# A batch-normalised outer product on one core: long rows stored in halves, part of their finishing moved to ScalarE and GpSimd, short rows moved to VectorE

## The chip, the core and the metric

The kernel runs on one core of a Trainium2 chip. A core has a matrix engine (PE), three engines for elementwise work, VectorE (DVE), ScalarE (ACT) and GpSimd (POOL), and a queue processor (SyncE, SP) that here issues the stores. SBUF is the working memory of 128 partitions; PSUM is a smaller memory that GpSimd does not use in this kernel. Sixteen DMA engines move data between SBUF and the chip's main memory (HBM). Instructions of one engine run in their order; engines wait for each other through semaphores.

The metric is the device time of one launch in microseconds. Before the change it is 1891.26 us, the median of 3 runs (1891.12 to 1891.61).

## The reference

`xi` and `xj` are 1024 x 39 x 16 floats. For each of the 741 pairs (r, c) with c < r the outer product of xj's feature r and xi's feature c is formed, normalised over the batch and the 16 x 16 entries, scaled by gamma and beta of the pair, and multiplied by a matrix W.

```python
rows, cols = np.tril_indices(39, k=-1)          # 741 pairs
cross = xj[:, rows, :, None] * xi[:, cols, None, :]           # 1024 x 741 x 16 x 16
mean = jnp.mean(cross, axis=(0, 2, 3), keepdims=True)
var = jnp.mean(jnp.square(cross - mean), axis=(0, 2, 3), keepdims=True)
normed = (cross - mean) * jax.lax.rsqrt(var + 1e-5)
normed = normed * gamma[None, :, None, None] + beta[None, :, None, None]
out = normed[:, :, None, :, :] * W[None, None, :, :, :]
```

The output holds 1024 x 741 x 256 floats, 777 MB; the inputs are 5 MB. For each pair the normalisation is one factor s and one summand t: out = (s * cross + t) * W.

## The kernel before

**Setup.** The batch is laid over the 128 partitions, 8 entries on each (NT = 8). From sums and products of xi and xj, without forming any pair, the kernel works out s and t of all pairs (lines 249 to 427); `apply` (line 423) combines them with gamma and beta, group of rows by group of rows, and leaves s in `st_sb[:, 0]` and t in `st_sb[:, 1]` (SBUF). `w_dve` is a copy of W in PSUM for VectorE, `w_sb` the one in SBUF for GpSimd.

**Tiles.** A row r has the r pairs (r, 0) to (r, r-1). A tile is one row for two of the 8 batch entries of each partition (T = 2), 2 x r x 256 floats a partition. `tiles` (lines 62 to 71) lists row 19 first, then for r = 20 to 38 and each of the four batch pairs the row r and its partner 38 - r, together 76 KB a partition. The buffer `y_sb` has two halves of that size, used in turn; a row and its partner share a half. Row 38 has no partner.

**A tile's way.** From the third tile on (the loop at line 438):

- `scale_xi` (line 155): GpSimd multiplies xi by s into a small buffer `xs`, of which there are two. It is issued two tiles ahead.
- `products` (line 167): for each of the two batch entries and each i of 16, one instruction multiplies `xs` by the scalar xj[r, i] and writes 16 of the 256 entries of all r pairs. Of the 16, ScalarE takes 12 and GpSimd 4; for rows over TWO = 31, ScalarE 11 and GpSimd 5. They write into `y_sb`, so they wait until the stores of what lay there have landed.
- `finish` (line 219): for all but the last pairs of the row, VectorE does t and W in one instruction a pair (line 238). The last 13% of the pairs, rounded, are GpSimd's: it adds t pair by pair (line 226) and multiplies all of them by W at once (line 230).
- `store` (line 175): SyncE issues the store when its pairs are finished. `bounds` (line 212) cuts a row into pieces: one for rows to ONE = 24, two for rows to TWO = 31, three above; the first eight tiles have cuts of their own. The last piece of a row over 24 goes as two stores, one for each batch entry, so that the products of the first entry can begin before the second has left.

The program's order on each engine is the order in the file: `finish` of tile n, then `products` of tile n + 1. The first two tiles take another way: products of raw xi, then s and t in one instruction (`affine`, line 186), then W on VectorE (`weigh`, line 200).

The step that the change touches on the long rows:

```python
split = r - int(r * POOL_SHARE + 0.5)
for c in range(split, r):
    nc.gpsimd.tensor_scalar(y[:, :, c, :], ..., t_c, 1.0, ALU.add, ALU.mult)
nc.gpsimd.tensor_tensor(y[:, :, split:r, :], ..., w_sb, ALU.mult)
```

Of the kernel before, what the change touches and what calls it, by code (L numbers as in the profile page):

```python
# [7 lines left out]
F32 = mybir.dt.float32  # L8
AF = mybir.ActivationFunctionType
ALU = mybir.AluOpType  # L10
# [4 lines left out]
T = 2  # L15


ONE, TWO = 24, 31
FIRST_PIECES = (
    (0, 2, 5, 9, 14, 19), (0, 6, 12, 19), (0, 4, 11, 19), (0, 9, 19), (0, 10, 20), (0, 9, 18), (0, 10, 20), (0, 9, 18)  # L20
)


POOL_I, POOL_I_LONG = 4, 5
POOL_SHARE = 0.13

LOADS = (0, 1, 2, 4, 8)


ROW_GROUPS = (  # L30
# [5 lines left out]
def tile_pair_outer_batchnorm(  # L36
# [15 lines left out]
    nc = tc.nc  # L52
    P = nc.NUM_PARTITIONS
    NB, F, E = xi.shape
    NT = NB // P
    EE = E * E
    NP = F * (F - 1) // 2
    first = [r * (r - 1) // 2 for r in range(F)]
# [5 lines left out]
    tiles = [(mid, t0, t0 // T * half // 2) for t0 in range(0, NT, T)]  # L64
# [8 lines left out]
    RAW = 2  # L73

    cpool = ctx.enter_context(tc.tile_pool(name="cpool", bufs=1))
    scaled = ctx.enter_context(tc.tile_pool(name="scaled", bufs=2))
    psp = ctx.enter_context(tc.tile_pool(name="ps", bufs=1, space=bass.MemoryType.PSUM))
    xi_sb = cpool.tile([P, NT, F, E], F32, name="xi_sb")
    xj_sb = cpool.tile([P, NT, F, E], F32, name="xj_sb")
    w_sb = cpool.tile([P, 1, EE], F32, name="w_sb")  # L80
    st_sb = cpool.tile([P, 2, NP], F32, name="st_sb")
    s_sb = st_sb[:, 0:1].unsqueeze(3)
    t_sb = st_sb[:, 1]
# [39 lines left out]
    banks = [psp.tile([P, 512], F32, name=f"ps{n}") for n in range(7)]  # L123
    ps_s, ps_c, ps_g = banks[0], banks[1], banks[2:5]

    ps_st = banks[5:7] + ps_g
    stt = nc.vector.scalar_tensor_tensor

    def view(n):
        r, _, u = tiles[n]  # L130
        return y_sb[:, u : u + T * r, :].rearrange("p (t n) e -> p t n e", t=T)

    def product(n, engine, t, i, src):

        r, t0, _ = tiles[n]
        y = view(n).rearrange("p t n (i j) -> p t n i j", j=E)[:, t, :, i, :]
        scale = xj_sb[:, t0 + t, r, i : i + 1]
        if engine is nc.scalar:
            nc.scalar.activation(y, src, AF.Copy, scale=scale)  # L139
        else:  # L140
            engine.tensor_scalar(y, src, scale, 1.0, ALU.mult, ALU.mult)  # L141
# [12 lines left out]

    def scale_xi(n):
        r, t0, _ = tiles[n]
        n0 = first[r]
        xs = scaled.tile([P, T, r, E], F32, tag="xs", name=f"xs_{r}_{t0}")
        nc.gpsimd.tensor_tensor(  # L159
            xs,  # L160
            xi_sb[:, t0 : t0 + T, 0:r, :],
            s_sb[:, :, n0 : n0 + r, :].to_broadcast([P, T, r, E]),
            ALU.mult,
        )
        xs_of[n] = xs

    def products(n):

        xs = xs_of.pop(n)
        split = E - (POOL_I_LONG if tiles[n][0] > TWO else POOL_I)  # L170
        for t in range(T):
            for i in range(E):
                product(n, nc.scalar if i < split else nc.gpsimd, t, i, xs[:, t])

    def store(n, c0, c1):
        r, t0, _ = tiles[n]
        n0 = first[r]

        step = 1 if r > ONE and c1 == r else T
        for t in range(0, T, step):  # L180
            nc.sync.dma_start(  # L181
                out_v[:, t0 + t : t0 + t + step, (n0 + c0) * EE : (n0 + c1) * EE],
                view(n)[:, t : t + step, c0:c1, :].rearrange("p t n e -> p t (n e)"),
            )

    def affine(n):

        r = tiles[n][0]
        y = view(n)
        for c in range(r):  # L190
            s_c = st_sb[:, 0, first[r] + c : first[r] + c + 1]
            t_c = t_sb[:, first[r] + c : first[r] + c + 1]
            if c % 2 == 0:
                nc.scalar.activation(y[:, :, c, :], y[:, :, c, :], AF.Identity, bias=t_c, scale=s_c)  # L194
            else:
                nc.gpsimd.tensor_scalar(  # L196
                    y[:, :, c, :], y[:, :, c, :], s_c, t_c, ALU.mult, ALU.add
                )

    def weigh(n):  # L200

        y = view(n)
        for c0, c1 in zip(bounds(n), bounds(n)[1:]):
            nc.vector.tensor_tensor(  # L204
                y[:, :, c0:c1, :],
                y[:, :, c0:c1, :],
                w_dve.unsqueeze(1).to_broadcast([P, T, c1 - c0, EE]),
                ALU.mult,
            )
            store(n, c0, c1)  # L210

    def bounds(n):
        if n < len(FIRST_PIECES):
            return FIRST_PIECES[n]
        r = tiles[n][0]
        pieces = 1 + (r > ONE) + (r > TWO)
        return tuple(q * r // pieces for q in range(pieces + 1))

    def finish(n):

        r = tiles[n][0]
        n0 = first[r]
        y = view(n)
        split = r - int(r * POOL_SHARE + 0.5)
        for c in range(split, r):
            nc.gpsimd.tensor_scalar(  # L226
                y[:, :, c, :], y[:, :, c, :], t_sb[:, n0 + c : n0 + c + 1], 1.0, ALU.add, ALU.mult
            )
        if split < r:
            nc.gpsimd.tensor_tensor(  # L230
                y[:, :, split:r, :],
                y[:, :, split:r, :],
                w_sb.unsqueeze(1).to_broadcast([P, T, r - split, EE]),
                ALU.mult,
            )
        for c0, c1 in zip(bounds(n), bounds(n)[1:]):
            for c in range(c0, min(c1, split)):
                stt(  # L238
                    y[:, :, c, :],
                    y[:, :, c, :],  # L240
                    t_sb[:, n0 + c : n0 + c + 1],
                    w_dve.to_broadcast([P, T, EE]),
                    ALU.add,
                    ALU.mult,
                )
            store(n, c0, c1)

    with tc.manual_schedule():
        for t0, t1 in zip(LOADS, LOADS[1:]):
            nc.sync.dma_start(xj_sb[:, t0:t1], xj_v[:, t0:t1])  # L250
# [157 lines left out]
        for r0, r1, bank, _ in ROW_GROUPS:  # L408
            n0, n1 = first[r0], first[r1 - 1] + r1 - 1
            at = used[bank]  # L410
            used[bank] = at + 2 * (n1 - n0)
            ps = ps_st[bank][:, at : used[bank]].rearrange("p (x n) -> p x n", x=2)
# [10 lines left out]
        def apply(group):  # L423
            ps, n0, n1 = spread_of[group]
            nc.vector.tensor_mul(ps[:, 1], ps[:, 1], st_sb[:, 0, n0:n1])
            nc.vector.tensor_mul(st_sb[:, 0, n0:n1], ps[:, 0], st_sb[:, 0, n0:n1])
            nc.vector.tensor_add(st_sb[:, 1, n0:n1], ps[:, 1], st_sb[:, 1, n0:n1])

        apply(0)
        affine(0)  # L430
        weigh(0)
        scale_xi(2)
        affine(1)
        weigh(1)
        apply(2)
        apply(1)

        for n in range(1, len(tiles)):
            if n == 1:
                products(2)  # L440
                scale_xi(3)
                continue
            if n + 2 < len(tiles):
                scale_xi(n + 2)
            finish(n)
            for group, (_, _, _, tile_of) in enumerate(ROW_GROUPS):
                if n == tile_of:
                    apply(group)
            if n + 1 < len(tiles):
                products(n + 1)  # L450
# [28 lines left out]
```

## Time and profile before

| | |
|---|---|
| time of the runs (median of 3) | 1891.26 us |
| the profiled execution's own time | 1891.05 us |
| its span (first to last instruction) | 1889.3 us |
| VectorE busy | 1730.7 us, 92% of the span |
| ScalarE busy | 1621.3 us, 86% |
| GpSimd busy | 1574.5 us, 83% |
| matrix engine busy | 24.5 us, 1% |
| time of the packets on the store queue | 98.3% of 16 engines' span |
| written to HBM | 777 MB, 414 GB/s with the reads over the span |
| stores issued | 305 |

Busy time is read as follows: an engine's instructions overlap a little, so the mean duration of VectorE's line 238, 740 ns, is more than their spacing; eleven of them in a row took 7.32 us, 0.67 us each. "Idle before, and releaser" names what ended a wait: line 139 on ScalarE waited 171.8 us in total for stores to land, in 58 waits. "issue" means that the profile shows nothing waited for. A slice of the page is a fortieth of the span, 47.2 us.

### The profile page before, as it was taken

The page shows a single profiled execution, that of the slowest core. Times are in us where ns is not written, and L with a number is a line of the kernel's source. Part 1 is how long each engine was busy: PE and PEld are TensorE (multiplying, and loading weights), DVE is VectorE, ACT ScalarE, POOL GpSimd, SP SyncE. Part 2 cuts the span into 40 slices and gives each one's busy share as a digit, 9 for nine tenths or more (in the row PEclk, how much of TensorE's full clock was granted, in tenths as well). Part 3 has the DMA queues.
Part 4 walks back from the last instruction along what each step waited for, and adds up shares of the span by engine and source line. Part 5 has one row for each costly group of instructions (what it writes and reads, how often), then busy time and mean ns, then how long its engine had stood idle before and what let it go on. Part 6 is the DMA issues. An engine that isn't in the chain of part 4 may idle for free. (4 is left out here: it accounts for less than half of the span.)

```text
span 1889.3 us, 10288 instructions
## 1 busy us (share of the span) xinstructions
PE 24.5 (1%) x128; PEld 23.1 (1%) x128; DVE 1730.7 (92%) x2612; ACT 1621.3 (86%) x3625; POOL 1574.5 (83%) x1985
## 2 busy tenths in 40 slices
PE   3100000000000000000000000000000000000000
PEld 3100000000000000000000000000000000000000
DVE  7999999998989898989898989899999999999996
ACT  8999989898989898989898989888888888888762
POOL 9798878788888888888888888888888888888972
DMA  4999999999999999999999999999999999999999
GB/s 164 390 418 429 425 427 429 430 424 429 424 425 426 424 424 426 422 425 425 424 425 423 426 423 426 422 422 422 421 421 422 418 415 419 416 419 419 415 419 390
DMA packets 70288, 783.67 MB, mean 415 GB/s; under 512 B 5057, under 2 KB 6209, under 8 KB 15937
## 3 DMA queue, kind: packets, MB, share of 16 engines
q1 hardware_dynamic: 69632, 780.46, 98.3%
q10 hardware_dynamic: 576, 2.56, 0.3%
q14 instruction: 79, 0.64, 0.1%
q8 instruction: 1, 0.02, 0.0%
HBM read 6.00 MB, written 776.99 MB: 414 GB/s over the span
## 5 line engine op out<-in xcount | busy, mean ns | idle before, releaser
L238 DVE SCALAR_TENSOR_TENSOR y_sb<-y_sb,st_sb,w_dve 128x512 f32<-128x512 f32 x2542 | 1678.5, 740 | 131.5 <-issue 128.3
L139 ACT ACTIVATE y_sb<-xs,xj_sb 128x256 f32<-128x256 f32 (+32 forms) x3544 | 1576.4, 539 | 223.5 <-DMA out_dram<-y_sb 171.8
L141 POOL TENSOR_SCALAR y_sb<-xs,xj_sb 128x560 f32<-128x560 f32 (+35 forms) x1256 | 643.2, 536 | 35.1 <-DMA out_dram<-y_sb 32.6
L230 POOL TENSOR_TENSOR y_sb<-y_sb,w_sb 128x1024 f32<-128x1024 f32 (+4 forms) x138 | 442.0, 3203 | 11.5
L159 POOL TENSOR_TENSOR xs<-xi_sb,st_sb 128x576 f32<-128x576 f32 (+37 forms) x150 | 187.8, 1252 | 225.3 <-ACT y_sb L139 217.8
L226 POOL TENSOR_SCALAR y_sb<-y_sb,st_sb 128x512 f32<-128x512 f32 x384 | 259.4, 692 | 12.9 <-ACT y_sb L139 12.9
L204 DVE TENSOR_TENSOR y_sb<-y_sb,w_dve 128x2560 f32<-128x2560 f32 (+5 forms) x8 | 21.0, 2682 | 2.3 <-ACT y_sb L194 2.3
L139 ACT ACTIVATE y_sb<-xi_sb,xj_sb 128x304 f32<-128x304 f32 x40 | 18.7, 534 | 0.1
L414 PE MATMUL ps<-y_sb 39*128 39x38 f32 (+37 forms) x76 | 16.5, 397 | 5.6 <-DVE y_sb L402 5.6
L414 PEld LDWEIGHTS ps<-y_sb 39*128 39x128 f32 x76 | 16.3, 329 | 5.8 <-issue 5.8
L194 ACT ACTIVATE y_sb<-y_sb,st_sb 128x512 f32<-128x512 f32 x20 | 14.2, 797 | 0.0
L196 POOL TENSOR_SCALAR y_sb<-y_sb,st_sb 128x512 f32<-128x512 f32 x18 | 13.5, 771 | 0.3 <-issue 0.3
L141 POOL TENSOR_SCALAR y_sb<-xi_sb,xj_sb 128x304 f32<-128x304 f32 x24 | 11.9, 518 | 0.0
L299 DVE TENSOR_REDUCE y_sb<-y_sb 128x78 f32<-128x1248 f32 x8 | 11.1, 1442 | 0.0
L277 DVE TENSOR_REDUCE y_sb<-xj_sb 128x78 f32<-128x1248 f32 (+1 forms) x5 | 5.9, 1189 | 5.6 <-DMA xj_sb<-in_r_xj_dram 5.6
L293 ACT ACTIVATE y_sb<-y_sb 128x1248 f32<-128x1248 f32 x8 | 9.9, 1243 | 1.3 <-POOL y_sb L283 1.1
L283 POOL TENSOR_TENSOR y_sb<-xj_sb,y_sb 128x1248 f32<-128x1248 f32 x4 | 9.3, 2314 | 1.9 <-ACT y_sb L327 1.9
L283 POOL TENSOR_TENSOR y_sb<-xi_sb,y_sb 128x1248 f32<-128x1248 f32 x4 | 9.3, 2318 | 0.0
L316 PE MATMUL ps<-y_sb 128*39 128x79 f32 x48 | 7.2, 339 | 16.5 <-DVE y_sb L299 16.5
L316 PEld LDWEIGHTS ps<-y_sb 128*39 128x39 f32 x48 | 6.1, 183 | 17.4 <-DVE y_sb L299 9.6
L277 DVE TENSOR_REDUCE y_sb<-xi_sb 128x78 f32<-128x1248 f32 (+1 forms) x5 | 5.9, 1186 | 0.0
L259 POOL TENSOR_SCALAR_AFFINE_SELECT y_sb<-y_sb 39x4992 f32<-39x4992 f32 x1 | 4.6, 4623 | 0.0
(45 smaller groups left out, 16.9 us busy)
## 6 DMA issues: line engine op xcount, KB each, us to landing
out_dram<-y_sb SPq DMA_DIRECT2D x32, 3072.0 KB, 13.7
out_dram<-y_sb SPq DMA_DIRECT2D x28, 2816.0 KB, 15.7
out_dram<-y_sb SPq DMA_DIRECT2D x32, 1664.0 KB, 14.2
out_dram<-y_sb SPq DMA_DIRECT2D x16, 3328.0 KB, 17.2
out_dram<-y_sb SPq DMA_DIRECT2D x30, 1536.0 KB, 15.2
out_dram<-y_sb SPq DMA_DIRECT2D x12, 3840.0 KB, 17.6
out_dram<-y_sb SPq DMA_DIRECT2D x12, 3584.0 KB, 18.1
out_dram<-y_sb SPq DMA_DIRECT2D x22, 1792.0 KB, 17.4
```

Of the source, the lines that this page charges most:

```text
L139: nc.scalar.activation(y, src, AF.Copy, scale=scale)
L141: engine.tensor_scalar(y, src, scale, 1.0, ALU.mult, ALU.mult)
L159: nc.gpsimd.tensor_tensor(xs, xi_sb[:, t0 : t0 + T, 0:r, :], s_sb[:, :, n0 : n0 + r, :].to_broadcast([P, T, r, E]), ALU.mult,)
L194: nc.scalar.activation(y[:, :, c, :], y[:, :, c, :], AF.Identity, bias=t_c, scale=s_c)
L196: nc.gpsimd.tensor_scalar(y[:, :, c, :], y[:, :, c, :], s_c, t_c, ALU.mult, ALU.add)
L204: nc.vector.tensor_tensor(y[:, :, c0:c1, :], y[:, :, c0:c1, :], w_dve.unsqueeze(1).to_broadcast([P, T, c1 - c0, EE]), ALU.mult,)
L226: nc.gpsimd.tensor_scalar(y[:, :, c, :], y[:, :, c, :], t_sb[:, n0 + c : n0 + c + 1], 1.0, ALU.add, ALU.mult)
L230: nc.gpsimd.tensor_tensor(y[:, :, split:r, :], y[:, :, split:r, :], w_sb.unsqueeze(1).to_broadcast([P, T, r - split, EE]), ALU.mult,)
L238: stt(y[:, :, c, :], y[:, :, c, :], t_sb[:, n0 + c : n0 + c + 1], w_dve.to_broadcast([P, T, EE]), ALU.add, ALU.mult,)
L283: nc.gpsimd.tensor_tensor(devs[n % 7], sources[x][:, t0 : t0 + T], shift[:, x : x + 1, :].unsqueeze(3).to_broadcast([P, T, F, E]), ALU.sub ...
L316: nc.tensor.matmul(acc[0:F, 0 : 2 * F + 1], lhs, fb[:, t], start=t == 0, stop=t == NT - 1)
L414: nc.tensor.matmul(ps[:, :, first[r] - n0 : first[r] - n0 + r], pick[:, r, :], stq[:, :, 0:r], start=True, stop=True,)
```

## The change

Four things are changed together.

1. `TWO` goes: rows over 24 are all cut in two pieces, so rows 32 to 38 leave in halves and not in thirds. The limit from which GpSimd takes 5 of 16 products moves from 31 to `LONG` = 33.
2. Rows over 33: the GpSimd pairs are no longer the last ones but the last eight of the first half (`p0` to `p1`), in two groups of four. ScalarE adds t to them, one instruction a pair; GpSimd multiplies each group by W. VectorE does all others.
3. Rows of up to 4 pairs (`SHORT`): `scale_xi` is left out; VectorE multiplies xi by s and forms the products, one instruction for each batch entry, and no pair is left to GpSimd.
4. For that, s and xj are also kept in PSUM: `apply` now leaves s in PSUM too and copies it to `st_sb` with an instruction of its own, and one ScalarE copy during setup puts xj of rows 1 to 4 into PSUM (`xj_short`).

```diff
-ONE, TWO = 24, 31
+ONE, LONG = 24, 33
-POOL_SHARE = 0.13
+POOL_SHARE, POOL_PAIRS_LONG = 0.13, 8
+SHORT = 4
...
+    s_short = ps_g[0]
+    xj_short = ps_c.rearrange("p (t r i) -> p t r i", t=NT, i=E)
...
     def scale_xi(n):
         r, t0, _ = tiles[n]
+        if r <= SHORT:
+            return
...
     def products(n):
+        r, t0, _ = tiles[n]
+        if r <= SHORT:
+            xs = scaled_short.tile([P, T, r, E], F32, tag="xs_short", name=f"xs_{r}_{t0}")
+            nc.vector.tensor_tensor(
+                xs,
+                xi_sb[:, t0 : t0 + T, 0:r, :],
+                s_short[:, first[r] : first[r] + r]
+                .unsqueeze(1)
+                .unsqueeze(3)
+                .to_broadcast([P, T, r, E]),
+                ALU.mult,
+            )
+            for t in range(T):
+                nc.vector.tensor_tensor(
+                    view(n)[:, t].rearrange("p n (i j) -> p n i j", j=E),
+                    xs[:, t].unsqueeze(2).to_broadcast([P, r, E, E]),
+                    xj_short[:, t0 + t, r - 1 : r, :].unsqueeze(3).to_broadcast([P, r, E, E]),
+                    ALU.mult,
+                )
+            return
         xs = xs_of.pop(n)
-        split = E - (POOL_I_LONG if tiles[n][0] > TWO else POOL_I)
+        split = E - (POOL_I_LONG if tiles[n][0] > LONG else POOL_I)
...
-        pieces = 1 + (r > ONE) + (r > TWO)
+        pieces = 1 + (r > ONE)
...
     def finish(n):
-        split = r - int(r * POOL_SHARE + 0.5)
-        for c in range(split, r):
-            nc.gpsimd.tensor_scalar(
-                y[:, :, c, :], y[:, :, c, :], t_sb[:, n0 + c : n0 + c + 1], 1.0, ALU.add, ALU.mult
-            )
-        if split < r:
+        long = r > LONG
+        p1 = r // 2 if long else r
+        p0 = p1 - (POOL_PAIRS_LONG if long else int(r * POOL_SHARE + 0.5) if r > SHORT else 0)
+        step = POOL_PAIRS_LONG // 2 if long else r
+        for c0 in range(p0, p1, step):
+            c1 = min(c0 + step, p1)
+            for c in range(c0, c1):
+                t_c = t_sb[:, n0 + c : n0 + c + 1]
+                if long:
+                    nc.scalar.activation(y[:, :, c, :], y[:, :, c, :], AF.Identity, bias=t_c)
+                else:
+                    nc.gpsimd.tensor_scalar(
+                        y[:, :, c, :], y[:, :, c, :], t_c, 1.0, ALU.add, ALU.mult
+                    )
             nc.gpsimd.tensor_tensor(
-                y[:, :, split:r, :],
-                y[:, :, split:r, :],
-                w_sb.unsqueeze(1).to_broadcast([P, T, r - split, EE]),
+                y[:, :, c0:c1, :],
+                y[:, :, c0:c1, :],
+                w_sb.unsqueeze(1).to_broadcast([P, T, c1 - c0, EE]),
                 ALU.mult,
             )
         for c0, c1 in zip(bounds(n), bounds(n)[1:]):
-            for c in range(c0, min(c1, split)):
+            for c in [*range(c0, min(c1, p0)), *range(max(c0, p1), c1)]:
                 stt(
...
         def apply(group):
             ps, n0, n1 = spread_of[group]
             nc.vector.tensor_mul(ps[:, 1], ps[:, 1], st_sb[:, 0, n0:n1])
-            nc.vector.tensor_mul(st_sb[:, 0, n0:n1], ps[:, 0], st_sb[:, 0, n0:n1])
+            nc.vector.tensor_mul(ps[:, 0], ps[:, 0], st_sb[:, 0, n0:n1])
+            nc.vector.tensor_copy(st_sb[:, 0, n0:n1], ps[:, 0])
             nc.vector.tensor_add(st_sb[:, 1, n0:n1], ps[:, 1], st_sb[:, 1, n0:n1])
 
         apply(0)
         affine(0)
+        nc.scalar.copy(xj_short, xj_sb[:, :, 1 : SHORT + 1, :])
         weigh(0)
```

In the built order this makes the products of rows 1 to 4 stand on VectorE after the long partner's pairs, and the eight adds on ScalarE directly after the row's own products. Rows 32 to 38 issue one store fewer a tile.

More of the change, by code (lines that the diff above doesn't have):

```diff
@@ L75, in tile_pair_outer_batchnorm @@
     cpool = ctx.enter_context(tc.tile_pool(name="cpool", bufs=1))
+    scaled_short = ctx.enter_context(tc.tile_pool(name="scaled_short", bufs=1))
     scaled = ctx.enter_context(tc.tile_pool(name="scaled", bufs=2))
```

## The prediction

> **What bounds the kernel now.** I read the page's slices first: is anything full?
>
> ```profile
> DVE  7999999998989898989898989899999999999996
> ACT  8999989898989898989898989888888888888762
> DMA  4999999999999999999999999999999999999999
> GB/s 164 390 418 429 425 427 429 430 424 429 424 425 426 424 424 426 422 425 425 424 425 423 426 423 426 422 422 422 421 421 422 418 415 419 416 419 419 415 419 390
> ```
>
> The DMA engines are full from the second slice on; VectorE is close behind. GB/s falls late, at full DMA. So I asked for busy time and rate in stretches that hold whole rows: 22 to 24, 25 to 31, 32 to 37, and 38 (columns: stretch, its length, busy us by engine, clock, DMA share, GB/s).
>
> ```profile
> 283.40:564.20 280.80, 0.00 (x0) 0.00 (x0) 262.01 (x399) 254.67 (x576) 233.77 (x300) 1.00 1.00 427
> 564.20:1224.00 659.80, 0.00 (x0) 0.00 (x0) 609.33 (x924) 592.47 (x1341) 547.15 (x703) 1.00 1.01 424
> 1224.00:1794.20 570.20, 0.00 (x0) 0.00 (x0) 520.10 (x788) 470.72 (x1076) 497.70 (x627) 1.00 1.00 419
> 1794.20:1888.20 94.00, 0.00 (x0) 0.00 (x0) 74.36 (x113) 41.39 (x60) 49.97 (x47) 1.00 0.97 409
> ```
>
> A unit is a row r and its partner 38-r, two batches each: 76 KB a partition, 9.96 MB. Per batch and partition it leaves in 2, 3 and 4 contiguous stretches in the first three windows, in 3 in the last. The times at which each store's completion lands in the trace, taken over whole rows, give per unit 23.40 us (rows 22 to 24), 23.56 us (25 to 31; single rows 23.41 to 23.69), 23.76 us (32 to 37; 23.68 to 23.86), 23.52 us (row 38). The rate follows the number of stretches.
>
> Then what has to keep that queue full: the chain of waits (start, length, what) in row 37, and the timeline there.
>
> ```profile
> 1742.58 3.88 ACT y_sb L139 x6
> 1746.46 0.21 issue
> 1746.67 1.98 ACT y_sb L139 x3
> 1748.65 5.93 DVE y_sb L238 x9
> 1754.64 11.12 DMA out_dram<-y_sb
> ...
> 1765.87 4.75 ACT y_sb L139 x7
> ```
>
> ```profile
> 1742.58 19.81 ACT L139 ACTIVATE y_sb<-xs,xj_sb 128x592 f32<-128x592 f32 x46 [4.50 <-DMA out_dram<-y_sb]
> ...
> 1757.73 10.62 DVE L238 SCALAR_TENSOR_TENSOR y_sb<-y_sb,st_sb,w_dve 128x512 f32<-128x512 f32 x16 [2.49 <-issue]
> ...
> 1760.03 3.35 POOL L226 TENSOR_SCALAR y_sb<-y_sb,st_sb 128x512 f32<-128x512 f32 x5
> 1763.46 5.62 POOL L230 TENSOR_TENSOR y_sb<-y_sb,w_sb 128x2560 f32<-128x2560 f32 x1
> ```
>
> It is a ring of two halves of y: a landing frees a half (1742.5), ScalarE's 22 products take 15 us, VectorE starts when they are done (1757.73), a third of the row is stored, that store waits in the queue. I call slack the time by which a first third's issue comes before the queue would run dry: landing of the store ahead, minus end of the issue, minus 1.8 us (the first store of all, into an empty queue, landed 3.25 us after its issue, of which its packets are 1.44). From the trace: row 32 7.3 to 8.4 us, 34 5.8 to 6.9, 35 5.2 to 5.9, 36 3.2 to 4.3, 37 2.5 to 3.4, row 38's four tiles 2.6, 2.3, 2.1, 1.4. Slack is thin exactly where the change works.
>
> **What the Trainium skill says.** "DMA: Bandwidth & Descriptors", Why small descriptors are slow, gives each packet a fixed overhead beside its bytes; the trace agrees: median packets take 427 ns for 11,264 B, 841 ns for 22,528 B, so two of the small cost 13 ns more than one of the large. "SBUF — State Buffer", Who interferes with whom: a VectorE instruction with at most one SBUF input doesn't contend with GpSimd; both new VectorE multiplies take the other input from PSUM, and line 238, built so, keeps 0.66 us a pair while GpSimd works. "ScalarE: Activation LUTs", What ACT_TABLE_LOAD costs, prices a per-partition pointer operand at some 93 ns: here 797 ns with two against 708 with one, same size.
>
> **Part by part.** Prices, from the groups by shape (busy us, mean ns of one):
>
> ```profile
> L230 POOL TENSOR_TENSOR y_sb<-y_sb,w_sb 128x2048 f32<-128x2048 f32 x10 | 45.1, 4513 | 0.8
> L194 ACT ACTIVATE y_sb<-y_sb,st_sb 128x512 f32<-128x512 f32 x20 | 14.2, 797 | 0.0
> L139 ACT ACTIVATE y_sb<-xs,xj_sb 128x512 f32<-128x512 f32 x29 | 18.0, 708 | 4.2 <-DMA out_dram<-y_sb 4.2
> ```
>
> And from the timeline of the start:
>
> ```profile
> 63.96 11.28 DVE L238 SCALAR_TENSOR_TENSOR y_sb<-y_sb,st_sb,w_dve 128x512 f32<-128x512 f32 x17 [1.44 <-ACT y_sb L139]
> ```
>
> *Halves instead of thirds, rows 32 to 38.* 7 rows x 8 batches x 128 partitions = 7,168 packets of 63,744 go, and 28 of 305 stores. By landings: 24 units x (23.76 - 23.56) + 4 x (23.52 - 23.40) = 5.3 us. By packets: row 38 had 465 + 2 x 502 ns; 19,456 B lies between 691 (18,432 B) and 766 (20,480 B), so 2 x 728; 12 ns less, 16 packets an engine and unit: 0.20 us x 28 = 5.6 us. By the windows: 24 x (23.77 - 23.49), from 9.96 MB at 419 and 424 GB/s, and 4 x (23.49 - 23.33) for row 38 at the rates of three and two stretches, 7.4 us, but they count bytes of engines that run ahead. I take 5.4; ends 3.5 and 7.4.
>
> *Eight pairs of rows 34 to 38.* The t-add moves from GpSimd to ScalarE: 8 a tile at 0.62 (one pointer, 18.0/29) to 0.71 us (14.2/20), say 5.2 us. GpSimd's weighing goes from one of 5 pairs (5.6, after 3.35 of adds) to two of 4 (4.51 each): 9.0 before, 9.0 after. VectorE is spared 3 to 4 pairs a tile, 0.66 us each. The chain matters: in the first half 4 adds (2.6) and two multiplies (9.0) with hand-overs make 11.8 us after the products; before, the first third was 12 x 0.66 = 7.9 us. So 3.9 later (4.5 in rows 34 and 35). Against it: the products of a half start when batch 0 of the last piece has landed, and what drains after that is batch 1 of 19 pairs, not 13: 6 x 128 KB, 1.9 us earlier (1.5 in row 34). Net 2.0 us later (3.0 and 2.6). Slack left: row 34 about 3, 35 about 2.9, 36 1.7, 37 1.0, row 38 0.6, 0.3, 0.1, -0.6. I charge 0.7 us. Behind the adds on ScalarE stand the next products: 22 x 0.67 + 5.2 = 20 us of 23.6, free in time.
>
> *Rows 32, 33.* 16 pairs before the first store instead of 10 or 11 (+3.3 to 4.0 us), one more ScalarE product a batch (+0.6 each), start 1.5 earlier: about 3.7 of 6.6 to 8.4 us slack. Nothing.
>
> *Rows 1 to 4.* ScalarE loses 24 products of 0.22 us (5.2 us: it pays for the adds), GpSimd 8. VectorE gains, for r = 4, one multiply of 128 and two of 1,024 elements (line 204 took 1,220 ns for 1,024): 2.7 us, and a pair of t and W (0.66), against 4 pairs spared (2.6). For r = 1 about 1.1 against 2. Equal; its gap of 2.49 us a unit covers it. They stand behind the long row's stores; the queue holds over 9 us then.
>
> *Setup.* A ScalarE copy of 512 elements before the second tile: 0.6 us by the product of that size. VectorE has weighing to do until 61.2, but at 63.96 it waits for ScalarE's products, and the store that follows (issue ended 67.21, store ahead landed 68.13) finds no slack: +0.6. Six extra copies in apply, 0.18 to 0.41 us by the multiplies of their shapes: the first lies under ScalarE's products (till 39.13), two under the 1.44 us wait, three where VectorE idles: +0.1, ends 0 and 0.9.
>
> Sum: -5.4 + 0.7 + 0.6 + 0.1 = -4.0. Span 1889.3 to 1885.3; the profiled execution itself 1891.05 to 1887.05; the median of the runs is 0.2 above that: **1887.2 us**, its own range 1884.6 to 1889.3.
>
> **Rivals.** *Gain half eaten*: hand-overs cost 0.9 us more a tile, rows 37 and 38 starve. A late first half delays every second unit (the other ring half then has the surplus): two payments a row, some 2 us: 1889.2. For it the thin slack; against it row 38 now, which runs on 1.4 to 2.6 us and still makes 23.52. *No gain in rate*: rows 32 to 37 are slow because the queue runs low, not for packets; then only +1.4: 1892.7. Against it DMA share 1.00 and slack above 5 in rows 32 to 34, as slow as the rest. *Slower*: the chain from ScalarE to GpSimd, twice over, decides. If it takes d longer than 11.8 us, each row pays 2 x (d - slack): for d = 2.7 that is 2 x (1.0 + 1.7 + 2.6) for rows 36, 37, 38, some 10.6 in place of 0.7: 1897. The sign turns at d = 1.7 (a multiply of 5.4 us instead of 4.51), 0.2% slower at 2.35. For it: spans on GpSimd are rough, and this chain was never on the path; against it 4.51 is the same shape in the same kernel. *The change does nothing*: excluded: in the built order rows 32 to 38 have one store fewer a tile, and the short rows' products stand on VectorE.
>
> **How the numbers follow.** Forecast 0.66, half eaten 0.12, no gain 0.06, slower chain 0.16. About 0.2% (3.8 us) is what a measurement here can tell. The forecast's middle lies just beyond it, so I count three fifths of that case as faster and the rest, with the two cases between, as no change: faster 0.40, same 0.44, slower 0.16. Range: the forecast's low end, and up to where half the slow case is in: 1884.5 to 1895.
>
> **What would show it.** Right: GB/s of the last nine slices near 424; about 62,000 packets on the first queue (69,632 - 7,168 - 28 x 16); line 267 at 4.5 us; first halves issued 0 to 3 us ahead of need; DMA share under 1 only in row 38. Wrong: line 267 above 5.3 us, or ScalarE's wait for the landing gone while VectorE waits longer; DMA slices below 9 from 1420 us on; or a rate that stays at 419 with a full queue.

## The result, and the profile after

The changed kernel takes 1885.37 us, the median of 6 runs (1885.22 to 1885.50); the kernel before took 1891.19 us on the same chip (6 runs, 1891.06 to 1891.61). The ratio is 0.9969, with a 95% interval of 0.9956 to 0.9982: 5.8 us or 0.31% less, a little more than the 0.2% that the prediction set as its bound. It forecast 1887.2 us, in a range of 1884.5 to 1895. The profiled execution took 1885.49 us, with a span of 1883.8.

First the slices of the page after the change, and the line of the store queue (packets, MB, share of 16 engines).

```profile
DVE  7999999998989898989898989898999999988885
ACT  8999989898989898989898989898988888888883
DMA  4999999999999999999999999999999999999999
GB/s 162 386 420 424 428 428 426 431 424 425 431 423 426 424 426 423 425 424 425 426 423 425 423 426 425 416 425 423 419 421 427 421 428 421 423 419 418 424 416 413
...
q1 hardware_dynamic: 62016, 780.46, 98.2%
```

The DMA engines are as full as before, and VectorE is less full at the end (8 where there was 9). The last nine slices run at 413 to 428 GB/s, 420 on average, where they ran at 390 to 419, 414 on average; the prediction named 424 as the sign of being right, and four of the last five slices stay short of it. The queue carries 62,016 packets, 7,616 fewer than before. Then busy time and rate in stretches that hold whole rows: 25 to 31, 32 to 37 and 38 (columns: stretch, its length, busy us of PE, PEld, DVE, ACT and POOL, clock, DMA share, GB/s).

```profile
564.20:1224.00 659.80, 0.00 (x0) 0.00 (x0) 608.65 (x923) 594.28 (x1344) 545.09 (x700) 1.00 1.01 424
1224.00:1790.00 566.00, 0.00 (x0) 0.00 (x0) 520.64 (x793) 483.17 (x845) 451.92 (x401) 1.00 1.00 422
1790.00:1882.00 92.00, 0.00 (x0) 0.00 (x0) 64.25 (x98) 54.01 (x80) 48.23 (x33) 1.00 0.99 423
```

Rows 25 to 31, which leave as they did, keep their 424. Rows 32 to 37 go from 419 to 422. Row 38 shows 409 before and 423 here, but the window before runs to the last landing and this one stops 0.9 us short of it: over the whole row, 1789.4 to 1882.9 us, it is 418. ScalarE has 12 us more to do in rows 32 to 37, GpSimd 46 us less.

The difference can be placed to a tenth of a microsecond with the times at which the stores' completions land in the trace, per unit (a row, its partner and two batches; 4 units a row). A row ends when the last of the 16 DMA engines has completed its last store:

| | before | after | difference in all |
|---|---|---|---|
| rows 25 to 31, us a unit | 23.564 | 23.560 | 28 x -0.004 = -0.1 |
| rows 32 to 37, us a unit | 23.760 | 23.537 | 24 x -0.223 = -5.4 |
| row 38, us a unit | 23.515 | 23.383 | 4 x -0.132 = -0.5 |
| last landing of row 19, us | 94.60 | 95.20 | +0.6 |
| end of the span after the last landing, us | 1.09 | 0.85 | -0.2 |

Together -5.6, which is the difference of the spans (1889.34 and 1883.78) within rounding (rows 20 to 24 add less than 0.1). So nearly all that was won was won where the rows leave in halves; the start lost 0.6. Row 38's 0.5 is the least certain part, since its end before is set by one engine that landed 1.1 us behind the other 15.

The timeline in row 37 shows the new hand-overs (start, length, what, count, wait and its releaser).

```profile
1736.19 15.05 ACT L145 ACTIVATE y_sb<-xs,xj_sb 128x592 f32<-128x592 f32 x22 [2.85 <-DMA out_dram<-y_sb]
...
1747.63 0.75 DVE L190 TENSOR_TENSOR y_sb<-xs,ps 128x256 f32<-128x256 f32 x2
...
1751.34 13.92 DVE L275 SCALAR_TENSOR_TENSOR y_sb<-y_sb,st_sb,w_dve 128x512 f32<-128x512 f32 x21 [2.17 <-ACT y_sb L145]
1751.34 5.01 ACT L262 ACTIVATE y_sb<-y_sb,st_sb 128x512 f32<-128x512 f32 x8
1754.04 9.02 POOL L267 TENSOR_TENSOR y_sb<-y_sb,w_sb 128x2048 f32<-128x2048 f32 x2 [4.44 <-ACT y_sb L262]
```

When the 22 products are done (1751.24), ScalarE adds t to eight pairs in 5.01 us; GpSimd starts after four of them, at 1754.04, and is done at 1763.06. The first half can be issued 11.8 us after the products, as the prediction had it. The short partner, row 1, sits on VectorE just before. The groups by shape over rows 34 to 38 (busy us, mean ns of one, idle before):

```profile
L267 POOL TENSOR_TENSOR y_sb<-y_sb,w_sb 128x2048 f32<-128x2048 f32 x40 | 180.1, 4525 | 94.5 <-ACT y_sb L262 94.5
L262 ACT ACTIVATE y_sb<-y_sb,st_sb 128x512 f32<-128x512 f32 x156 | 97.7, 708 | 1.8
...
L190 DVE TENSOR_TENSOR y_sb<-xs,ps 128x1024 f32<-128x1024 f32 x8 | 9.4, 1218 | 0.1
```

The chain of waits in the same stretch of row 37 (start, length, what) has the order that it had before: weighing on VectorE, with the short row behind it, a landing, ScalarE's products.

```profile
1740.84 6.66 DVE y_sb L275 x10
1747.50 0.03 DVE xs L180
1747.53 11.83 DMA out_dram<-y_sb
...
1759.46 6.52 ACT y_sb L145 x10
```

The shares have moved, though: from 1715 to 1790 us the chain is 45% ScalarE's products, 37% VectorE's pairs and 16% stores, where from 1720 to 1800 us before it was 31, 27 and 42%. The ring has less room than it had.

The slack of the first piece (the prediction's measure) fell as the halves and the chain through GpSimd imply: row 34 from 5.8-6.9 to 2.1-3.3 us, 36 from 3.2-4.3 to 1.2-2.6, 37 from 2.5-3.4 to 0.3-1.9, and row 38 from 2.6, 2.3, 2.1, 1.4 to 0.6, 1.2, -0.8, -0.4.

### The profile page after: what moved, and what is told of

Its sections match the earlier page's. It is cut to its first block, busy times and chain, and to the rows that moved or that the text cites. A ratio compares the mean times of both kernels' runs of the same rounds, so it can differ in the third digit from the quotient of the medians.

```text
span 1883.8 us, 9616 instructions
## 1 busy us (share of the span) xinstructions
PE 24.5 (1%) x128; PEld 23.1 (1%) x128; DVE 1721.6 (91%) x2606; ACT 1648.8 (88%) x3418; POOL 1524.4 (81%) x1741
## 3 DMA queue, kind: packets, MB, share of 16 engines
q1 hardware_dynamic: 62016, 780.46, 98.2%
## 5 line engine op out<-in xcount | busy, mean ns | idle before, releaser
L275 DVE SCALAR_TENSOR_TENSOR y_sb<-y_sb,st_sb,w_dve 128x512 f32<-128x512 f32 x2482 | 1640.5, 741 | 131.0 <-issue 117.7
L145 ACT ACTIVATE y_sb<-xs,xj_sb 128x320 f32<-128x320 f32 (+20 forms) x3176 | 1503.1, 566 | 192.2 <-DMA out_dram<-y_sb 165.4
L147 POOL TENSOR_SCALAR y_sb<-xs,xj_sb 128x352 f32<-128x352 f32 (+25 forms) x1112 | 597.8, 561 | 41.0 <-DMA out_dram<-y_sb 36.4
L267 POOL TENSOR_TENSOR y_sb<-y_sb,w_sb 128x2048 f32<-128x2048 f32 (+3 forms) x154 | 509.4, 3313 | 104.0 <-ACT y_sb L262 94.5
L167 POOL TENSOR_TENSOR xs<-xi_sb,st_sb 128x576 f32<-128x576 f32 (+33 forms) x134 | 182.7, 1364 | 185.2 <-ACT y_sb L145 179.1
L264 POOL TENSOR_SCALAR y_sb<-y_sb,st_sb 128x512 f32<-128x512 f32 x284 | 192.1, 692 | 0.1
L262 ACT ACTIVATE y_sb<-y_sb,st_sb 128x512 f32<-128x512 f32 x160 | 100.2, 708 | 1.9
L190 DVE TENSOR_TENSOR y_sb<-xs,ps 128x1024 f32<-128x1024 f32 (+3 forms) x32 | 24.8, 817 | 0.5
L222 ACT ACTIVATE y_sb<-y_sb,st_sb 128x512 f32<-128x512 f32 x20 | 14.3, 798 | 0.0
L224 POOL TENSOR_SCALAR y_sb<-y_sb,st_sb 128x512 f32<-128x512 f32 x18 | 13.5, 763 | 0.6 <-issue 0.6
```

Of the source, the lines that this page charges most:

```text
L167: nc.gpsimd.tensor_tensor(xs, xi_sb[:, t0 : t0 + T, 0:r, :], s_sb[:, :, n0 : n0 + r, :].to_broadcast([P, T, r, E]), ALU.mult,)
L190: nc.vector.tensor_tensor(view(n)[:, t].rearrange("p n (i j) -> p n i j", j=E), xs[:, t].unsqueeze(2).to_broadcast([P, r, E, E]), xj_short ...
L264: nc.gpsimd.tensor_scalar(y[:, :, c, :], y[:, :, c, :], t_c, 1.0, ALU.add, ALU.mult)
L267: nc.gpsimd.tensor_tensor(y[:, :, c0:c1, :], y[:, :, c0:c1, :], w_sb.unsqueeze(1).to_broadcast([P, T, c1 - c0, EE]), ALU.mult,)
L275: stt(y[:, :, c, :], y[:, :, c, :], t_sb[:, n0 + c : n0 + c + 1], w_dve.to_broadcast([P, T, EE]), ALU.add, ALU.mult,)
```

## The experiments

The theory, **P** in the expectations: what was won is packets. A stretch less per batch and partition is 16 packets less on each DMA engine and unit, and with a full queue each packet has a fixed price. Rivals: **V**, the relief of VectorE and GpSimd wins; **S**, the number of stores counts and not that of packets. Beside these, the prediction's own terms: the price of a late first half, and of the copy at the start. Each kernel ran beside the kernel before on the same chip; "before" was 1891.04 us for the first four runs, 1891.19 for the next four, 1891.07 for the last two.

One table for all, by landings, in us a unit:

| kernel | stretches in rows 32 to 37 | rows 25 to 31 | rows 32 to 37 | row 38 | median of runs, us |
|---|---|---|---|---|---|
| before | 4 | 23.564 | 23.760 | 23.515 | 1891.19 |
| after | 3 | 23.560 | 23.537 | 23.383 | 1885.37 |
| halves alone | 3 | 23.564 | 23.563 | 23.577 | 1886.57 |
| all but the halves | 4 | 23.567 | 23.731 | 23.524 | 1890.84 |
| halves as two stores | 3 | 23.557 | 23.536 | 23.334 | 1885.06 |
| one group of eight | 3 | 23.560 | 23.651 | 24.286 | 1891.53 |
| quarters | 5 | 23.562 | 23.926 | 23.708 | 1895.94 |
| without the eight pairs | 3 | 23.564 | 23.787 | 23.579 | 1892.43 |
| without the short rows | 3 | 23.566 | 24.329 | 23.856 | 1905.53 |
| late copy | 3 | 23.565 | 23.530 | 23.375 | 1884.80 |
| late copy, six pairs | 3 | 23.560 | 23.559 | 23.351 | 1885.01 |
| the same, rows 25 and 26 whole | 3 | 23.544 | 23.549 | 23.349 | 1884.37 |

**Halves alone.** The kernel before with one edit:

```diff
-        pieces = 1 + (r > ONE) + (r > TWO)
+        pieces = 1 + (r > ONE)
```

> The kernel before with one edit: rows 32 to 38 leave in halves; GpSimd's pairs, the short rows and the setup stay as they were. Theory P (the gain is the 7,168 packets less, as long as the queue never runs dry): rows 32 to 37 at 23.54 us a unit, row 38 near 23.4; the first half takes VectorE 19 x 0.66 = 12.5 us instead of 11.8, so 0.7 us less slack than the full change and about 1 us more starving in rows 37 and 38, but no 0.6 us in the setup: about 1886, at most 1 us from the changed kernel. Rival V (the gain is that VectorE has fewer pairs in rows 34 to 38): no gain here, 1891 or more.

Measured: 1886.57 us, ratio 0.9976 (0.9967 to 0.9986): 4.5 of the 5.8 us come from this one edit, with VectorE's and GpSimd's shares as they were. V falls. The queue shows as many packets as after the change, 62,016. What is missing lies in rows 34 (23.664), 36 (23.601) and 38 (23.577); the other rows are as fast as after the change. In row 38 the slack is -0.5, -0.7, -0.7 and -1.5 us.

**All but the halves.** The changed kernel with thirds:

```diff
-        pieces = 1 + (r > ONE)
+        pieces = 1 + (r > ONE) + (r > 31)
```

> The changed kernel, but rows 32 to 38 leave in thirds as before; the eight pairs, the short rows and the setup stay changed. P: units of rows 32 to 37 back at 23.76 us, the setup's 0.6 us remains: 1891.8. V: the gain stays, about 1886.

Measured: 1890.84 us, ratio 0.9999 (0.9991 to 1.0008). Without the halves nothing is left of the gain, though VectorE and ScalarE work as in the changed kernel and slack in row 34 is 6.0 to 7.1 us. Seen from both sides, then, the halves are the gain. It came 1.0 us lower than expected: its rows 32 to 37 take 23.731 us a unit and not 23.76 (0.7 of it), and row 19's last landing is 0.3 us earlier than after the change.

**Halves as two stores.** The first halves of rows over 31 also go as two stores, one for each batch entry: 305 stores as before, packets as after (62,464 on the queue, 16 more for each store).

```diff
-        step = 1 if r > ONE and c1 == r else T
+        step = 1 if r > 31 or (r > ONE and c1 == r) else T
```

> The changed kernel; in rows 32 to 38 the first half too goes as two stores, one for each batch entry: 305 stores again, the same data packets as the changed kernel. P: 28 stores x 16 completion packets of 9 ns on 16 engines are 0.25 us: 1885.6. Rival S (a store has a cost of its own, and 28 fewer stores are the gain): near 1891.

Measured: 1885.06 us, ratio 0.9968 (0.9956 to 0.9980). The gain stays although no store was saved. S falls: 28 stores more cost nothing that shows.

**Quarters.** The dose the other way, rows 32 to 38 in four pieces:

```diff
-        pieces = 1 + (r > ONE)
+        pieces = 1 + (r > ONE) + 2 * (r > 31)
```

> The changed kernel, rows 32 to 38 in four pieces: two stretches a batch more than halves. P, dose and response: each stretch cost 0.20 us a unit, 28 units, two of them: +11 us, 1896.5, units of rows 32 to 37 near 23.95 us. If finer pieces helped the queue more than packets cost: below 1885.

Measured: 1895.94 us, ratio 1.0025 (1.0015 to 1.0036), 10.6 us above the changed kernel. With 3, 4 and 5 stretches a unit of rows 32 to 37 takes 23.54 (after), 23.73 to 23.76 (thirds, before) and 23.93 us: some 0.20 us a stretch. The first of these fences is of the changed kernel, the second of the one with quarters, both the window over rows 32 and 33:

```profile
1230.00:1410.00 180.00, 0.00 (x0) 0.00 (x0) 166.54 (x253) 160.32 (x355) 149.85 (x181) 1.00 1.00 422
```

```profile
1230.00:1410.00 180.00, 0.00 (x0) 0.00 (x0) 162.65 (x247) 155.33 (x346) 146.28 (x179) 1.00 1.01 418
```

DMA is full in both, the slack with quarters is larger (7.4 to 8.6 us in row 32), and the rate is lower all the same. This is not a queue that runs dry.

**One group of eight.** GpSimd weighs the eight pairs at once, so it starts only after all eight adds: the chain to the first half gets longer, and nothing else changes.

```diff
-        step = POOL_PAIRS_LONG // 2 if long else r
+        step = POOL_PAIRS_LONG if long else r
```

> The changed kernel, but GpSimd weighs the eight pairs of rows 34 to 38 in one instruction after all eight adds: 5.0 + 8.9 = 13.9 us after the products instead of 2.5 + 9.0, 2.3 us later. By the ring's rule (a late first half costs its lateness beyond the slack, twice a row) with the slacks measured after the change, 2.8, 2.4, 1.9, 1.0 and -0.1: 2 x (0.4 + 1.3 + 2.3) = 8 us, 1893. If the first half's time did not matter (queue deep enough): 1885.4.

Measured: 1891.53 us, ratio 1.0003 (0.9994 to 1.0012): 6.5 us above the kernel with two stores that ran beside it. The timeline of a tile of row 37:

```profile
1728.52 5.01 ACT L262 ACTIVATE y_sb<-y_sb,st_sb 128x512 f32<-128x512 f32 x8
1733.67 8.87 POOL L267 TENSOR_TENSOR y_sb<-y_sb,w_sb 128x4096 f32<-128x4096 f32 x1 [6.05 <-ACT y_sb L262]
```

From the adds to the end of the weighing it is 14.0 us instead of 11.7. Nearly all of the cost is in rows 37 (24.075, slack -0.6 to -1.0) and 38 (24.286, slack -1.0 to -1.8); row 36 (slack -1.4 to 0.3) pays 0.16 us a unit, rows 34 and 35 (slack -0.3 to 1.0) nothing. So the slower rival's mechanism exists, and a chain 2.3 us longer takes the whole gain. Its price was set about 1.5 us too high.

**Without the eight pairs.** Rows over 33 end as the shorter ones do (GpSimd's 13% last); the rest of the change stays.

```diff
-        long = r > LONG
+        long = False
```

> The changed kernel without the eight pairs: in rows 34 to 38 GpSimd adds and weighs the last 4 or 5 pairs as before; halves, VectorE's short rows and setup stay. VectorE then has, for row 34, 30 pairs, 2.7 us of products and 4 pairs, 25.2 us a unit of 23.5: bound by VectorE there, less so in rows 35 to 37 (24.3, 24.0, 23.0 and up). By pure sum: 4 x (1.7 + 0.8 + 0.5) = 12 us, with waits at the start of each tile perhaps 25: 1897 to 1911. If the eight pairs are only there for the first half's time: about 1886.

Measured: 1892.43 us, ratio 1.0006 (0.9997 to 1.0016), 7 us more than with the eight pairs. The windows over row 34 and row 35:

```profile
1412.00:1508.00 96.00, 0.00 (x0) 0.00 (x0) 95.72 (x142) 57.11 (x89) 66.83 (x65) 1.00 0.96 405
1508.00:1605.00 97.00, 0.00 (x0) 0.00 (x0) 96.72 (x148) 57.88 (x88) 72.82 (x68) 1.00 0.98 412
```

VectorE, the third figure after the length, has no gap left: 95.72 of 96.0 us. It is the bound in these rows, where its partners have 4 and 3 pairs and it does them all. The expected loss was larger (1897 to 1911). Row 34 was charged 1.7 us a unit and pays 0.34: its slack falls from 4.0 us at the end of row 33 to -2.4 at the start of row 35, so most of what VectorE was behind there came out of the work in store. Row 35, charged 0.8, pays 0.71, and from row 36 on VectorE nearly keeps up again (23.70 and 23.73 us a unit).

**Without the short rows.** The eight pairs stay, rows 1 to 4 go the old way, over ScalarE and GpSimd. (The copy of xj at the start is kept.)

```diff
-SHORT = 4
+SHORT = 0
```

> The changed kernel, but rows 1 to 4 keep their products on ScalarE and GpSimd as before; the eight pairs and halves stay. ScalarE then has 14.6 + 5.0 + 5.2 = 24.8 us a unit of 23.5 in rows 34 to 37: 16 x 1.3 = 21 us, 1906 or somewhat more, ScalarE without idle time there. If ScalarE has room: 1885 to 1886.

Measured: 1905.53 us, from two runs (1904.62 and 1906.44), ratio 1.0075 (1.0055 to 1.0096), as expected. Its chain of waits in row 36:

```profile
1608.71 13.45 ACT y_sb L145 x20
...
1622.25 5.02 ACT y_sb L262 x8
1627.27 2.60 ACT y_sb L145 x13
...
1629.94 10.45 ACT y_sb L145 x23
```

ScalarE alone carries the chain: products, adds, the short row's 24 products, products. Over rows 34 to 37 it is busy 386.5 of 388 us, and the DMA share is 0.95. The two parts are each other's counterpart: the adds load ScalarE with what the short rows take off it, the short rows load VectorE with what the eight pairs take off it. One without the other costs 7 or 20 us.

**Late copy.** The copy of xj for short rows, which the prediction charged with 0.6 us, is issued in the loop instead of the setup, where it runs at 216 us:

```diff
-        nc.scalar.copy(xj_short, xj_sb[:, :, 1 : SHORT + 1, :])
...
                 if n == tile_of:
                     apply(group)
+                    if group == 4:
+                        nc.scalar.copy(xj_short, xj_sb[:, :, 1 : SHORT + 1, :])
```

> The changed kernel; the ScalarE copy of xj for rows 1 to 4 is issued in the loop, where the last group is applied, instead of during setup. The setup's cost as predicted was 0.6 us: 1884.8. If that shift came from the extra copies in apply instead, or is absorbed later: 1885.3 or above.

Measured: 1884.80 us, ratio 0.9966 (0.9953 to 0.9978), 6.4 us below the kernel before on its chip, where the changed kernel is 5.8 below. First the timeline of the start of the changed kernel, then that of this one:

```profile
46.28 0.57 ACT L469 COPY ps<-xj_sb 128x512 f32<-128x512 f32 x1
...
64.59 15.89 DVE L275 SCALAR_TENSOR_TENSOR y_sb<-y_sb,st_sb,w_dve 128x512 f32<-128x512 f32 x24 [1.39 <-ACT y_sb L145]
```

```profile
63.98 16.55 DVE L275 SCALAR_TENSOR_TENSOR y_sb<-y_sb,st_sb,w_dve 128x512 f32<-128x512 f32 x25 [0.86 <-ACT y_sb L145]
```

A copy of 0.57 us at 46.28 makes VectorE start its third tile 0.61 us later, 18 us further on; the last landing of row 19 is at 94.67 us without it and 95.20 with it. In all traces together that landing lies at 94.83 to 95.28 us in the seven kernels with the copy in the setup and at 94.38 to 94.67 in the five without. All of it reaches the end: 0.57 us between the medians.

**Six pairs instead of eight**, with the late copy: two groups of three shorten the chain, and VectorE gets two pairs a tile back.

```diff
-POOL_SHARE, POOL_PAIRS_LONG = 0.13, 8
+POOL_SHARE, POOL_PAIRS_LONG = 0.13, 6
```

> The changed kernel with the late copy, and six pairs in place of eight, in groups of three: 1.9 + 2 x 3.44 = 8.8 us and hand-overs after the products instead of 11.8; VectorE has 12 or 13 pairs before the half is out, 8.2 us. The first half is 3 us earlier, the two last tiles of row 38, 0.8 and 0.3 us late, are in time; VectorE carries two pairs more a unit, 22.8 of 23.5 us. If starving in row 38 costs what the ring's rule says, up to 1 us is won on the late copy alone: 1884.0. If VectorE is too full with two pairs more: 1885 to 1888.

Measured: 1885.01 us, ratio 0.9968 (0.9957 to 0.9980): nothing won. The timeline in row 38:

```profile
1798.01 3.78 ACT L262 ACTIVATE y_sb<-y_sb,st_sb 128x512 f32<-128x512 f32 x6
1800.29 6.83 POOL L267 TENSOR_TENSOR y_sb<-y_sb,w_sb 128x1536 f32<-128x1536 f32 x2
```

From the adds to the end of the weighing it is 9.1 us, and slack in row 38 is 2.7 to 3.3 us instead of -0.8 to 1.3 with the late copy alone. Row 38 takes 23.351 us a unit instead of 23.375, 0.1 us in all; rows 34 to 37 are even 0.04 a unit slower. The thin slack of the changed kernel cost next to nothing.

**Rows 25 and 26 whole**, on top of that: two stretches instead of three in 8 units.

```diff
-        pieces = 1 + (r > ONE)
+        pieces = 1 + (r > 26)
```

> The kernel of the run beside it (late copy, six pairs), and rows 25 and 26 leave whole: 2 rows x 1,024 packets less, the last piece still as two stores. P: 8 units x 0.17 us = 1.3 us, less what starves: the first store comes 6.6 us later, 2 to 3.7 of it won back by the earlier start, against 6 to 10 us of slack: some 1 us faster, 1883.0. If the whole row comes too late, rows 25 and 26 are over 23.6 us a unit and nothing is won.

Measured: 1884.37 us, ratio 0.9965 (0.9951 to 0.9979), the fastest kernel of the study; it beats the kernel before by 6.7 us and the one with six pairs beside it by 0.64. Rows 25 and 26 take 23.428 and 23.619 us a unit, against 23.494 and 23.638; over rows 25 to 31 together, 28 x (23.560 - 23.544) = 0.45 us are won, where 8 units at 0.20 would give 1.6. The rows behind them change too, up and down (28 by +0.22, 29 by -0.16, 27 by -0.10). The windows over rows 25, 26 and half of 27 show where it went, first with six pairs alone, then in this kernel:

```profile
564.20:800.00 235.80, 0.00 (x0) 0.00 (x0) 219.53 (x334) 216.67 (x489) 197.55 (x255) 1.00 1.01 425
564.20:800.00 235.80, 0.00 (x0) 0.00 (x0) 219.86 (x335) 217.25 (x490) 197.75 (x255) 1.00 1.00 424
```

With larger packets the rate should have risen, as in rows 22 to 24, which leave in two stretches at 427 GB/s; it fell, and with it the DMA share. The slack in rows 25 and 26, 5.8 to 10.2 us with six pairs, is -0.8 to 3.5 here: it fell by the whole delay (6.3 to 7.0 us a tile), and none of the 2 to 3.7 us came that were to be won back by the earlier start. So the queue ran low there. How much of the missing 1.2 us this takes, and why the rows behind change, stays open.

## Why the prediction was right, and which term was off

**The bound and the mechanism** were right. The prediction read a full queue whose rate follows the number of stretches, and took the gain from that. Halves alone give most of it, all but the halves give none, stores don't matter, and a fifth stretch costs what the fourth did. It also fits what the Trainium skill says in "DMA: Bandwidth & Descriptors", Why small descriptors are slow, of a fixed overhead for each packet. The page calls joining descriptors into packets worth it only at 256 B and below; here, where the pieces themselves are longer and fewer, with packets of 10 to 20 KB, 0.20 us a unit over 16 packets of an engine is still 12.5 ns each, and it shows at a DMA share of 1.00.

**The size of the halves.** Forecast -5.4, from three estimates of 5.3, 5.6 and 7.4. Measured -5.4 in rows 32 to 37 and -0.5 in row 38: -5.9, 0.5 of the miss. The estimate by packets was the best one, and better still with its sum put right: 465 + 2 x 502 is 1469 ns and 2 x 728 is 1456, so 13 ns less and not 12, 0.21 us a unit, 5.8 us in all. The packets of 19,456 B, which the kernel before did not have, take 728 ns in the trace after, as was read between their neighbours.

**Starving in rows 37 and 38** is the term that failed: "Slack left: row 34 about 3, 35 about 2.9, 36 1.7, 37 1.0, row 38 0.6, 0.3, 0.1, -0.6. I charge 0.7 us." The slacks came (row 34 2.1 to 3.3, 36 1.2 to 2.6, 37 0.3 to 1.9, row 38 0.6, 1.2, -0.8, -0.4), the charge did not: with 3 us of slack given back, row 38 gained 0.1 us. The runs put the point at which a unit pays lower than zero: against the row with 3 us of slack, a unit of row 38 loses 0.02 us at a slack of -0.8 to 1.3 (late copy), 0.2 at -0.5 to -1.5 (halves alone) and 0.9 at -1.0 to -1.8 (one group). Slack alone doesn't give the price: row 37 of the one-group kernel pays 0.55 at -0.6 to -1.0. The 1.8 us that the measure sets off for the way from issue to landing came from a store into an empty queue and may be too long for this use; that was not tried by itself. The measure also goes by the last of the 16 engines to land. Taken by the mean of their completions, a unit of row 38 is 23.62 us with the late copy and 23.52 with six pairs: the average engine does lose 0.10 us, the last one 0.02. It fits that engines ahead of the others wait for a late store while the last one still has work (more on this at the end).

**The chain through GpSimd** was right: 11.8 us after the products, one multiply 4.53 us against 4.51. The rival that was slower had its mechanism right, as one group of eight shows, but its condition (a multiply above 5.3 us) did not come. Its turning point was put at 1.7 us more; with the price as measured it is about 2.3, where that kernel stands level with the one before.

**Short rows and the eight adds** were forecast as equal on VectorE and as paid for on ScalarE. Right: with both, the queue stays full in rows 32 to 37 (DMA share 1.00), though the chain of waits runs mostly through the two engines; take one away and the share falls to 0.96 in row 34 (without the eight pairs) or 0.95 in rows 34 to 37 (without the short rows). Beside the halves, the two together are worth 1.5 us (1886.57 for halves alone and 1885.06 for the kernel with two stores beside it), net of the copy at the start. The prediction gave them no gain; it has its place in rows 34, 36 and 38, where halves alone run short.

**Setup.** +0.6 for the copy: measured 0.6 at the last landing of row 19, and gone with the late copy. The +0.1 for the copies in `apply` doesn't show (row 32 starts 0.55 us later than before, less than the 0.6 that the copy explains).

**The sum.** -4.0 forecast for the span, -5.6 measured: 0.7 for starving, 0.5 for the halves, 0.15 for the setup, and 0.24 because the end follows the last landing more closely. That last part doesn't go with the packets (with two stores, which has the same data packets, it is 1.09 us again), no term of the prediction stood for it, and it is luck. The median of the runs was taken to lie 0.2 above the profiled execution; it lies 0.1 below. Together these are the 1.8 us between 1887.2 and 1885.37. The other rivals are out: "half eaten" needs rows 37 and 38 to pay, "no gain in rate" needs rows 32 to 37 at 23.76.

## What to carry to other kernels

When the output queue is full, look at how many separate stretches each partition writes, not at how many stores are issued: cutting 4 to 3 was worth 0.20 us of every 23.7 here, and only where the first piece still comes in time. Moving work from one engine to another needs its counterpart: each of the two moves here is a loss by itself, because it fills the engine it goes to. A short instruction added where a full queue is not yet covered by work in store, 0.57 us in the setup, goes to the end in full; the same instruction 170 us later costs nothing that shows.

## What the hardware showed that was not expected

- Stores were issued up to 0.8 us later than the measure of slack allows, and nothing that could be measured was lost.
- The 16 engines of one queue drift apart, and draw level when the queue runs low. At the end of the kernel before, 15 of the 16 engines' completions of the last store had come by 1887.16 us, and the last one at 1888.25, 1.1 us behind; after the change all 16 came within 0.2 us (1882.75 to 1882.93). The cut does not decide it: with the late copy they come within 0.2 us, with six pairs and the same cut from 1879.64 to 1882.49. What goes with it is the slack of the last tile of row 38: in the seven kernels where that is negative (-0.3 to -1.8 us) the completions lie within 0.2 us, in the five where it is 1.4 to 2.8 they lie 1.2 to 3.6 us apart. So a late store may cost the engines that are ahead and not the one that is last, which sets the landing; that would be why 0.8 us of lateness cost nothing. It follows from comparing the traces, and no run was made for it.
- Neighbouring rows of the same cut differ, and do so alike in every kernel but the last: row 28 takes 23.40 to 23.45 us a unit, row 29 23.67 to 23.69. Where rows 25 and 26 left whole, it was 23.65 and 23.52. So it isn't the row's size that decides, but something carried from row to row; its cause is open.
